# Gated window attention in one core: normalising in the input tile, transposes beside the maxima, mask first in the scores, key weights turned first, last output tile in two parts

## The chip, the cores and the metric

The kernel runs on one core of a Trainium2 chip. A core has five engines with a queue of their own: TensorE (PE in the profile; its weight loads are PEld), VectorE (DVE), ScalarE (ACT), GpSimd (POOL) and SyncE (SP), which here only issues DMAs. Matmuls write to PSUM, eight banks of 128 partitions x 512 f32. The metric is the device time of one execution in microseconds; less is better. Before the change it is 2263.09 us (median of 3 runs, 2261.22 to 2267.27).

## What is computed

For 8 sequences of 1024 tokens with 512 features, in f32:

```python
xn = (x - mean(x)) / sqrt(var(x) + 1e-5)
q, k, v = (heads(xn @ W.T + b) for W, b in ((Wq, bq), (Wk, bk), (Wv, bv)))   # 16 heads of 32
scores = q @ k.T / sqrt(32)
im = arange(1024) % 256
scores = where(im[:, None] >= im[None, :], scores, -1e30)
attn = softmax(scores) @ v
s = attn @ Wo.T + bo
y = clip((xn @ sign(weights).T) * scale + bias, -100, 100)
out = x + s * silu(y)
```

The mask goes by the place in a window of 256, not by the token's own place: a query sees, in each of the four windows, the keys up to its own place there.

## The kernel before

**Tiles.** Tokens are loaded so that a tile of 128 holds 32 places of all four windows (`tokens`, L124). In this order the mask is triangular over tiles: query tile i needs the key tiles 0 to i, and only the tile on the diagonal needs a mask inside. A batch has 8 tiles (`it`), 4 groups of 4 heads (`g`), and two halves of 4 tiles.

**Scores, twice.** For each batch and group the scores are made twice, each time in 9 quads: tiles of 4 banks, one bank a head, 4 heads side by side on 32 rows of TensorE each. There is one quad in PSUM (`ps_q`, one buffer), and all quads share it in turn.
- `maxima_quad` (L463, tile `s`): queries on partitions, keys along columns. S_QUADS says which queries and keys stand in each quad. The diagonal tile is masked by a product of two small bf16 matrices, `place_of` and `after` (L480), added to the scores in PSUM. VectorE takes the row maxima (L492). Five of the nine quads hold a diagonal; three of these hold two segments and two masks. The f32 product is L470.
- `shift_parts` and `shift_rows` split the maxima into three bf16 parts and transpose them (L519).
- `probs_quad` (L535, tile `t`): keys on partitions. First the shift is subtracted by a bf16 matmul (L541), then come the masks (L552), then the f32 product (L563). ScalarE takes Exp into a tile `p` (L576).
- `attend_quad` (L589) multiplies p with v into `av`; `add_probs` (L607) sums p on POOL; `sum_keys` (L630) sums over the keys; `invert` and `normalise_heads` divide (L664, L668).

**One step** of the main loop (from L948) is: the t quad of (b, g, n), the attend of the step before, a first fill, the s quad of the next group with the same n, a second fill. The fills are work that has nothing to do with the quad: projections q and k (`heads_work`), v (`values_work`), output tiles (`output_work`), gates (`gate_work`), transposes of xn (`turn` in `norm_work`). They keep TensorE at work while ScalarE does Exp (first fill) and VectorE the maxima (second fill). Two single banks (`ps_t`, `bank`) serve all of the fills, the turned maxima and the key sums.

**The plan.** The order of the fill is written out by hand in STEADY, OPENING and CLOSING (L726 to L743), one string for each group: V is a v tile, q20 the first half of q for group 2, k likewise, G a gate, O an output tile of the batch before, N the normalisation of a half of the next batch, W a turn of wo, a stroke marks work for the next batch, and what stands ahead of | may be taken early. Each word becomes a Block; `link` hangs smaller pieces on blocks some places away: an N at block i has its statistics at i - 5 and later (L777), its scale at i - 2 + half (L780), its normalising at i + half + 1 and later (L778), its turns at i + half + 2 + k (L779); a gate has its squash and finish behind it (L802, L803), an output tile its fetch one block ahead (L795). A `Work` has a cost (0.86 for a quarter of a product) and may be marked `edge` (run at the end of a fill, next to the quad), `late` (run at the end of the step) or `turn`. `Beside.fill` (L844) takes work from the front of the list until the wanted cost is reached. Work of cost 0 in the first fill is kept until after the s quad.

**Norms.** `stats` (L268) runs on VectorE, `scale` makes 1/sqrt on VectorE and POOL (L273 to L279), `normalise` makes xn in a buffer of the pool `tmp` (VectorE for the first batch, L284; ScalarE for the others, L289), and `turn` transposes it on TensorE into a bank (L301) that ScalarE copies into xnT (L302). `tmp` has 6 buffers of 128 x 512; gates (y, t), output tiles (s) and others draw on it too. `xpool` has 4 buffers for loaded tiles of x.

**Gates and outputs.** A gate's y is finished on POOL (L405, L406), for the last six (H in CLOSING) on VectorE; silu is made with Tanh, and the result g is stored to DRAM (L416). `output_work` fetches g and x again (L678, L680) into three buffers (`xres`), adds bo on VectorE (L686), multiplies by g and adds x on POOL (L688, L689; the last tile on VectorE) and stores (L690).

**Queues.** All loads of x, g and the stores go through SP in program order, so one that waits for a buffer or a result holds those behind it. In the opening wk and the biases go through ScalarE's queue.

**Beginning and end.** From L899: statistics of the first four tiles of x, normalise and turn them, turn wk (its copies alternate between VectorE and ScalarE, `evacuate` L223), then k, wq, q and so on, then the nine s quads of the first group with fill. From L1020: the last attend, then eight output tiles in the order 4 to 7, 0 to 3.

Of the kernel before, what the change touches and what calls it, by code (L numbers as in the profile page):

```python
# [9 lines left out]
F32 = mybir.dt.float32  # L10
# [7 lines left out]
B = 8  # L18
# [55 lines left out]
def tile_gated_window_attention(  # L74
# [23 lines left out]
    xpool = pool("xpool", 4)  # L98
# [7 lines left out]
    tmp = pool("tmp", 6)  # L106
# [123 lines left out]
    def turn_weight(name):  # L230


        def turn(c):
# [5 lines left out]
            ps = bank(f"{name}T_{c}")  # L239
# [4 lines left out]
            if name == "fw":  # L244

                sg = temp(f"sign_{c}")
                nc.vector.tensor_scalar(sg, ps, 0.0, 2.0, ALU.is_ge, ALU.mult)
                nc.vector.tensor_scalar(dst[:, c, :], sg, -1.0, None, ALU.add)
            elif name == "wo":

                nc.scalar.mul(dst[:, c, :], ps, 0.5)
            else:
                evacuate(dst[:, c, :], ps)
# [4 lines left out]
    xnT, turned = {}, set()  # L258

    def norm_work(b, half):  # L260
        its = range(4 * half, 4 * half + 4)
        mv, rstd, shift_by, xn = {}, {}, {}, {}
# [8 lines left out]
        def scale():  # L271
            rstd[0] = small.tile([P, 4], F32, tag="rstd", name=f"rstd_{b}_{half}")
            nc.vector.tensor_scalar(rstd[0], mv[0][:, :, 1], EPS, None, ALU.add)  # L273
            nc.gpsimd.tensor_tensor(rstd[0], rstd[0], neg_half, ALU.pow)
# [6 lines left out]
        def normalise(i, it):  # L281
            xn[it] = temp(f"xn_{b}_{it}")
            if b == 0:
                nc.vector.tensor_scalar(  # L284
                    xn[it], xt.pop((b, it)), mv[0][:, i, 0:1], rstd[0][:, i : i + 1],
                    ALU.subtract, ALU.mult,
# [3 lines left out]
                xn[it], xt.pop((b, it)), AF.Identity,  # L290
                bias=shift_by[0][:, i : i + 1], scale=rstd[0][:, i : i + 1],
            )

        def turn(i, it):
# [4 lines left out]
            x = xn.pop(it)  # L299
# [87 lines left out]
    def gate_work(b, it, plain=False):  # L387
# [13 lines left out]
        def after(ps):  # L401
            y[0] = temp(f"y_{b}_{it}")
            nc.vector.tensor_tensor(y[0], ps, rows["fscale"], ALU.mult)  # L403
            engine = nc.vector if plain else nc.gpsimd
            engine.tensor_tensor(y[0], y[0], rows["fbias"], ALU.add)  # L405
            engine.tensor_scalar(y[0], y[0], MAX_VAL, -MAX_VAL, ALU.min, ALU.max)  # L406
# [29 lines left out]
        if plain:  # L436
# [9 lines left out]
            Work(1.0, lambda: passes(0), edge=True),  # L446
            Work(1.0, lambda: passes(1), ready=lambda: bool(hold)),
        ]
        return split, [Work(2.0, both, lambda part: halves, edge=True)], squash, finish
# [13 lines left out]
    def maxima_quad(b, g, n):  # L463
        sc = quad(f"s_{b}_{g}_{n}")
        at = 0
        for i, lo, hi in S_QUADS[n]:
            own = lo <= i * P < hi
            w = hi - lo
            for h in range(NH):
# [4 lines left out]
                    start=(at == 0),  # L474
                    stop=not own,
                    skip_group_check=True,
                )
            if own:
                for h in range(NH):
                    nc.tensor.matmul(  # L480
                        sc[:, h, at + w - P : at + w],
                        lhsT=place_of[head_rows(h), :],
                        rhs=after[head_rows(h), :],
                        start=False,
                        stop=True,
                        skip_group_check=True,
                    )
# [187 lines left out]
    def output_work(b, it):  # L675
# [7 lines left out]
        def after(ps):  # L683
# [3 lines left out]
            engine = nc.vector if (b, it) == (B - 1, NT // 2 - 1) else nc.gpsimd  # L687
            engine.tensor_tensor(s, s, gb, ALU.mult)  # L688
            engine.tensor_tensor(s, s, xr, ALU.add)  # L689
            nc.sync.dma_start(tokens(out, b, it), s)  # L690

        main = product(
            f"o_ps_{b}_{it}",
            [
                (lambda g=g: (aT[b, g, it // 4][:, (it % 4) * P : (it % 4 + 1) * P], wT["wo"][:, g, :]))
                for g in range(NC)
            ],
            0.86,
            after,
        )  # L700
        return fetch, main

    def row_work():
# [7 lines left out]
        def after(ps):  # L711
# [3 lines left out]
            "bo_ps", [(lambda c=c: (wide[0][:, c, :], wT["wo"][:, c, :])) for c in range(NC)], 0.86, after  # L715
# [11 lines left out]
        "V4 G2 V5 | q20 V7 G3 V6 k20 q21 G4 k21",  # L727
        "O4 G5 O5 | q30 N0 k30 O6 q31 G6 k31 G7",
        "N1 O7 O0 | O1 k00' V0' q00' O2 q01' O3",
# [4 lines left out]
        "G3 G4 q20 G5 | N0 q30 k30 q31 G6 k31",  # L734
# [344 lines left out]
```

## Time and profile before

| what | value |
|---|---|
| median of the runs | 2263.09 us |
| the profiled execution | 2264.33 us |
| its span, first to last instruction | 2262.5 us |
| mean granted clock of TensorE | 0.997 |
| busy: TensorE, POOL, VectorE, ScalarE | 2200, 1467, 1208, 879 us |
| DMA moved | 93.51 MB, 41 GB/s over the span |
| Exp of one quad (L576) | 1.88 us |
| maxima of one quad of 4 x 512 (L492) | 2.29 us |
| one addition of 128 x 512 on POOL (L688) | 1.28 us |
| normalising one tile on ScalarE (L289) | 0.80 us |
| wait of TensorE for VectorE's first xn | 12.3 us |
| steady batch, from one to the next | 273.5 us |

The share of TensorE is that of time in which at least one matmul is in flight. Four matmuls of different heads run at once, so the starts of instructions tell more than their durations: the time that a group of matmuls takes from the stream is from its first start to the next group's first start. In the timeline's lines the columns are start, duration, engine, source line, operation, output<-inputs, shapes and number of instructions; in brackets stands the engine's idle time before it and what ended it. An f32 matmul shows as two instructions.

### The profile page before, as it was taken

The page shows a single profiled execution, that of the slowest core. Times are in us where ns is not written, and L with a number is a line of the kernel's source. Part 1 is how long each engine was busy: PE and PEld are TensorE (multiplying, and loading weights), DVE is VectorE, ACT ScalarE, POOL GpSimd, SP SyncE. Part 2 cuts the span into 40 slices and gives each one's busy share as a digit, 9 for nine tenths or more (in the row PEclk, how much of TensorE's full clock was granted, in tenths as well). Part 3 has the DMA queues.
Part 4 walks back from the last instruction along what each step waited for, and adds up shares of the span by engine and source line. Part 5 has one row for each costly group of instructions (what it writes and reads, how often), then busy time and mean ns, then how long its engine had stood idle before and what let it go on. Part 6 is the DMA issues. An engine that isn't in the chain of part 4 may idle for free.

```text
span 2262.5 us, 55901 instructions
## 1 busy us (share of the span) xinstructions
PE 2200.1 (97%) x25376; PEld 862.6 (38%) x25376; DVE 1207.5 (53%) x1535; ACT 879.2 (39%) x861; POOL 1467.1 (65%) x1291
## 2 busy tenths in 40 slices
PE   7999999999999999999999999999999999999998
PEld 3343433343433434333343333344333443333333
DVE  4555455564456544466455654555545664555563
ACT  2244433344333434344333443344344343333332
POOL 1367566776776766687567775667766676665663
PEclk9999999999999999999999999999999999999999
DMA  4001000121001210012000210002100111000123
GB/s 163 1 16 34 11 11 24 48 67 39 11 29 52 68 38 6 29 66 72 20 29 20 76 48 20 29 20 76 48 20 29 39 57 62 11 20 25 44 76 99
DMA packets 51087, 93.51 MB, mean 41 GB/s; under 512 B 6945, under 2 KB 6945, under 8 KB 50849
## 3 DMA queue, kind: packets, MB, share of 16 engines
q1 hardware_dynamic: 48720, 88.89, 11.9%
q8 instruction: 198, 3.24, 0.6%
q10 hardware_dynamic: 2128, 1.06, 0.2%
q14 instruction: 41, 0.33, 0.0%
HBM read 56.37 MB, written 33.55 MB: 40 GB/s over the span
## 4 chain that ended last, share of the span: by engine, by line
PE 83%; DVE 6%; ACT 4%; POOL 4%; issue 2%; DMA 1%; SPq 0%; ACTq 0%; POOLq 0%; DVEq 0%
PE s L470 13%; PE av L589 11%; PE t L563 10%; PE q_ps L331 9%; PE v_ps L331 9%; PE k_ps L331 9%; PE o_ps L331 7%; PE y_ps L425 5%; PE t L541 4%; DVE pm L492 4%; ACT p L576 2%; POOL p L607 2%; PE sum L630 2%; PE xnT_ps L301 2%; PE mT_ps L519 1%
## 5 line engine op out<-in xcount | busy, mean ns | idle before, releaser
L607 POOL TENSOR_TENSOR p<-p,p 128x512 f32<-128x512 f32 x930 | 1097.3, 1213 | 165.8 <-PE av L589 112.9
L492 DVE TENSOR_REDUCE pm<-s 128x4 f32<-128x2048 f32 (+3 forms) x384 | 665.1, 1753 | 709.9 <-PE s L480 462.6
L576 ACT ACTIVATE p<-t 128x2048 f32<-128x2048 f32 x288 | 540.8, 1878 | 760.8 <-PE t L563 684.7
L664 DVE RECIPROCAL aT<-aT 128x128 f32<-128x128 f32 x256 | 231.0, 929 | 242.8 <-ACT aT L625 242.8
L470 PE MATMUL s<-k,q 32*128 32x512 f32 (+3 forms) x3072 | 340.2, 528 | 15.4 <-ACT p L576 14.6
L589 PE MATMUL av<-p,v 128*32 128x512 f32 (+3 forms) x3072 | 308.7, 497 | 1.9 <-DVE aT L668 1.7
L563 PE MATMUL t<-q,k 32*128 32x512 f32 (+3 forms) x3072 | 305.6, 492 | 0.0
L331 PE MATMUL q_ps<-xnT,wqT 128*32 128x512 f32 (+3 forms) x2768 | 257.1, 486 | 4.5 <-ACT xnT L302 4.1
L331 PE MATMUL k_ps<-xnT,wkT 128*32 128x512 f32 (+3 forms) x2784 | 254.6, 483 | 0.3 <-ACT q L371 0.2
L331 PE MATMUL v_ps<-wvT,xnT 128*32 128x512 f32 (+3 forms) x2600 | 251.9, 505 | 0.0
L331 PE MATMUL o_ps<-woT,aT 128*32 128x512 f32 (+3 forms) x2480 | 249.1, 524 | 0.7 <-ACT xnT L302 0.7
L688 POOL TENSOR_TENSOR s<-s,gb 128x512 f32<-128x512 f32 x63 | 83.1, 1319 | 212.6 <-DVE s L686 211.5
L405 POOL TENSOR_TENSOR y<-y,fbias_r 128x512 f32<-128x512 f32 x58 | 76.4, 1317 | 201.8 <-DVE y L403 171.5
L399 POOL TENSOR_TENSOR x<-xnT,x 128x512 fp32r<-128x512 f32 x58 | 74.2, 1280 | 173.7 <-ACT x L398 169.9
L470 PEld LDWEIGHTS s<-k,q 32*128 32x128 f32 x3072 | 120.4, 183 | 134.2 <-ACT p L576 114.2
L563 PEld LDWEIGHTS t<-q,k 32*128 32x128 f32 x3072 | 138.4, 185 | 26.4
L331 PEld LDWEIGHTS q_ps<-xnT,wqT 128*32 128x32 f32 x2768 | 82.3, 110 | 170.9 <-issue 150.1
L589 PEld LDWEIGHTS av<-p,v 128*32 128x32 f32 x3072 | 70.3, 108 | 196.1 <-issue 161.1
L331 PEld LDWEIGHTS k_ps<-xnT,wkT 128*32 128x32 f32 x2784 | 83.5, 110 | 149.5 <-issue 125.2
L331 PEld LDWEIGHTS v_ps<-wvT,xnT 128*32 128x32 f32 x2600 | 75.1, 109 | 154.4 <-issue 139.1
L331 PEld LDWEIGHTS o_ps<-woT,aT 128*32 128x32 f32 x2480 | 74.0, 110 | 157.0 <-issue 144.8
L425 PE MATMUL y_ps<-fwT,x 128*128 128x512 f32 x464 | 129.4, 412 | 2.9 <-ACT q L371 2.9
(89 smaller groups left out, 1520.2 us busy)
## 6 DMA issues: line engine op xcount, KB each, us to landing
x<-in_L_attn_x_dram SPq DMA_DIRECT2D x64, 256.0 KB, 3.8
g<-t SPq DMA_DIRECT2D x64, 256.0 KB, 2.0
gb<-g SPq DMA_DIRECT2D x64, 256.0 KB, 3.0
xb<-in_L_attn_x_dram SPq DMA_DIRECT2D x64, 256.0 KB, 3.2
out_dram<-s SPq DMA_DIRECT2D x64, 256.0 KB, 2.5
wk_st<-in_L_attn_Wk_dram ACTq DMA_DIRECT2D x2, 512.0 KB, 4.6
wq_st<-in_L_attn_Wq_dram SPq DMA_DIRECT2D x2, 512.0 KB, 5.0
wv_st<-in_L_attn_Wv_dram SPq DMA_DIRECT2D x2, 512.0 KB, 6.6
```

Source lines behind the costliest of these rows:

```text
L331: nc.tensor.matmul(hold[0][cols, lo:hi], lhsT=lhsT[:, cols], rhs=rhs[:, lo:hi], start=(i == 0 and lo == 0), stop=(i == n - 1), skip_group_ ...
L405: engine.tensor_tensor(y[0], y[0], rows["fbias"], ALU.add)
L425: nc.tensor.matmul(hold[0], lhsT=part[i][:, c, :], rhs=wT["fw"][:, c, :], start=(i == 0 and c == 0), stop=(i == 1 and c == NC - 1),)
L470: nc.tensor.matmul(sc[:, h, at : at + w], lhsT=qt[b, g][head_rows(h), i * P : (i + 1) * P], rhs=kt[b, g][head_rows(h), lo:hi], start=(at = ...
L492: nc.vector.tensor_reduce(pm[:, 0 if lo == 0 else 1, i, :], sc[:, :, at : at + w], AX.X, ALU.max)
L541: nc.tensor.matmul(sc[:, h, at : at + w], lhsT=neg1[r, :], rhs=shift[b, g, f][r, lo : lo + w], start=(k == 0), stop=False, skip_group_chec ...
L563: nc.tensor.matmul(sc[:, h, at : at + w], lhsT=kt[b, g][head_rows(h), j * P : (j + 1) * P], rhs=qt[b, g][head_rows(h), q0 : q0 + w], start ...
L576: nc.scalar.activation(pt[:, :, :width], sc[:, :, :width], AF.Exp, scale=SCALE)
L589: nc.tensor.matmul(av[b, g, f][head_rows(h), lo : lo + w], lhsT=vt[b, j][:, g * P + h * DK : g * P + (h + 1) * DK], rhs=pts[b, g, n][:, h, ...
L607: nc.gpsimd.tensor_tensor(t[:, hs, lo : lo + w], t[:, hs, lo : lo + w], p[:, hs, at : at + w], ALU.add)
L664: nc.vector.reciprocal(r, r)
L688: engine.tensor_tensor(s, s, gb, ALU.mult)
```

## The change

- `normalise` writes xn back into the loaded tile of x. The tile is free when it has been turned, not when it has been normalised; `xpool` gets 5 buffers, `tmp` 5 in place of 6. A later load of x is ready only when the tile whose place it needs has been turned, a turn only when its tile is normalised.
- `scale` runs on POOL alone, and in the opening for two tiles at a time. For the second half of a batch statistics, scale and loads hang on other blocks.
- A turn is not run in a first fill, and at most one in a second. `fill` puts aside what is not ready if it is a turn or has no cost, and goes on with what follows; a product or a gate that is not ready ends the fill. Output tiles and gates get conditions (`ready`) of their own.
- The masks of an s quad are issued ahead of its f32 products, with the start flag.
- wk is turned ahead of everything else, into the four banks of the quad, and copied by ScalarE alone.
- The strings change: in STEADY q20 may be taken early, and O3 goes ahead of q01'; OPENING is rearranged. Turns of wo are marked `edge`. A gate's finish hangs one block earlier.
- The last gates use POOL as the others do. The last output tile has a function of its own: bo x g is added to x on POOL, the matmuls run in two halves of 256 columns, each is multiplied and added on VectorE and stored, one through SP, one through ScalarE's queue.

```diff
-    xpool = pool("xpool", 4)
+    xpool = pool("xpool", 5)
...
-    tmp = pool("tmp", 6)
+    tmp = pool("tmp", 5)
...
+            if name == "wk":
+
+                wide[0] = wide[0] or quad("wkT")
+                ps = wide[0][:, c, :]
+            else:
+                ps = bank(f"{name}T_{c}")
...
+            elif name == "wk":
+                nc.scalar.copy(dst[:, c, :], ps)
...
-        def scale():
-            rstd[0] = small.tile([P, 4], F32, tag="rstd", name=f"rstd_{b}_{half}")
-            nc.vector.tensor_scalar(rstd[0], mv[0][:, :, 1], EPS, None, ALU.add)
-            nc.gpsimd.tensor_tensor(rstd[0], rstd[0], neg_half, ALU.pow)
+        def scale(lo=0, hi=4):
+            if lo == 0:
+                rstd[0] = small.tile([P, 4], F32, tag="rstd", name=f"rstd_{b}_{half}")
+            r = rstd[0][:, lo:hi]
+            nc.gpsimd.tensor_scalar(r, mv[0][:, lo:hi, 1], EPS, None, ALU.add)
+            nc.gpsimd.tensor_tensor(r, r, neg_half[:, lo:hi], ALU.pow)
...
         def normalise(i, it):
-            xn[it] = temp(f"xn_{b}_{it}")
+            x = xt[b, it]
+            normed.add((b, it))
...
             nc.scalar.activation(
-                xn[it], xt.pop((b, it)), AF.Identity,
-                bias=shift_by[0][:, i : i + 1], scale=rstd[0][:, i : i + 1],
+                x, x, AF.Identity, bias=shift_by[0][:, i : i + 1], scale=rstd[0][:, i : i + 1]
             )
...
-            x = xn.pop(it)
+            x = xt.pop((b, it))
+            normed.discard((b, it))
...
-            engine = nc.vector if plain else nc.gpsimd
-            engine.tensor_tensor(y[0], y[0], rows["fbias"], ALU.add)
-            engine.tensor_scalar(y[0], y[0], MAX_VAL, -MAX_VAL, ALU.min, ALU.max)
+            nc.gpsimd.tensor_tensor(y[0], y[0], rows["fbias"], ALU.add)
+            nc.gpsimd.tensor_scalar(y[0], y[0], MAX_VAL, -MAX_VAL, ALU.min, ALU.max)
...
     def maxima_quad(b, g, n):
         sc = quad(f"s_{b}_{g}_{n}")
+        at, fresh = 0, False
+        for i, lo, hi in S_QUADS[n]:
+            w = hi - lo
+            if lo <= i * P < hi:
+                for h in range(NH):
+                    nc.tensor.matmul(
+                        sc[:, h, at + w - P : at + w],
+                        lhsT=place_of[head_rows(h), :],
+                        rhs=after[head_rows(h), :],
+                        start=not fresh,
+                        stop=False,
+                        skip_group_check=True,
+                    )
+                fresh = True
+            at += w
...
-                    start=(at == 0),
-                    stop=not own,
+                    start=not fresh,
+                    stop=True,
...
+    def last_output(b, it):
+
+        gb, xr = back.pop(it)
+        row = temp("row")
+        nc.gpsimd.tensor_tensor(row, gb, rows["bo"], ALU.mult)
+        nc.gpsimd.tensor_tensor(xr, xr, row, ALU.add)
+        s = temp(f"s_{b}_{it}")
+        ps = bank(f"o_ps_{b}_{it}")
+        for part, queue in enumerate((nc.sync, nc.scalar)):
+            at = slice(part * 256, part * 256 + 256)
+            for g in range(NC):
+                for h in range(NH):
+                    cols = head_rows(h)
+                    nc.tensor.matmul(
+                        ps[cols, at],
...
+            nc.vector.tensor_tensor(s[:, at], ps[:, at], gb[:, at], ALU.mult)
+            nc.vector.tensor_tensor(s[:, at], s[:, at], xr[:, at], ALU.add)
+            queue.dma_start(tokens(out, b, it)[:, :, at], s[:, at])
...
-        "V4 G2 V5 | q20 V7 G3 V6 k20 q21 G4 k21",
+        "V4 G2 V5 q20 | V7 G3 V6 k20 q21 G4 k21",
         "O4 G5 O5 | q30 N0 k30 O6 q31 G6 k31 G7",
-        "N1 O7 O0 | O1 k00' V0' q00' O2 q01' O3",
+        "N1 O7 O0 | O1 k00' V0' q00' O2 O3 q01'",
...
-        "G3 G4 q20 G5 | N0 q30 k30 q31 G6 k31",
-        "G7 N1 V0' V1' | W0 k00' W1 q00' W2 V2' W3 V3' q01'",
+        "G3 q20 q30 N0 k30 | G4 q31 G5 k31 G6 V0'",
+        "G7 N1 V1' | k00' q00' W0 V2' W1 V3' W2 q01' W3",
...
-                    link(i - 5 + 2 * half + k // 2, Work(0, stats[k], late=True))
+                    done = lambda key=(b + 1, 4 * half + k): key in normed
+                    link(i - 5 + (2 + k // 2 if half else 0) + k // 2, Work(0, stats[k], late=True))
                     link(i + half + max(1, k), normalise[k])
-                    link(i + half + 2 + k, Work(0.5, turn[k], turn=True))
-                link(i - 2 + half, Work(0, scale, late=True))
+                    link(i + half + 2 + k, Work(0.5, turn[k], turn=True, ready=done))
+                link(i - 2 + 2 * half, Work(0, scale, late=True))
...
-                link(i + 4 + later, finish)
+                link(i + 3 + later, finish)
...
-                    at = n0 + 4 + max(1, k)
-                    link(at, lambda b=b, it=4 + k: load_x(b + 1, it), True)
+
+                    ready = lambda key=(b + 1, k - 1): key[1] < 0 or key in turned
+                    fn = lambda b=b, it=4 + k: load_x(b + 1, it)
+                    link(n0 + 5 + k, Work(0, fn, ready=ready), True)
...
-                if not w.ready():
-                    if put_off:
-                        break
+                free = w.cost == 0
+                if not (free or w.turn or w.ready()):
                     while edge:
                         edge.pop(0).run()
-                if w.turn and (put_off or turns < 1):
+                if not w.ready() or free and waits or w.turn and turns < 1:
+                    if not (free or w.turn):
+                        break
+                    waits = waits or free
+                    turns = 0 if w.turn else turns
                     put_off.append(self.work.pop(0))
                     continue
...
+    for fn in turn_weight("wk"):
+        fn()
+    stats, scale, normalise, turn = norms[0]
+    for k in range(0, 4, 2):
+        stats[k]()
+        stats[k + 1]()
+        scale(k, k + 2)
+        normalise[k]()
+        normalise[k + 1]()
+    for k in range(4):
+        turn[k]()
     for w in heads_work(0, 0, 0, "k"):
         w.run()
+    stats, scale = norms[1][:2]
+    for k in range(0, 4, 2):
+        stats[k]()
+        stats[k + 1]()
+        scale(k, k + 2)
...
-                        want - spent, late, *kept, early=one is not now, turns=not (kept and turn)
+                        want - spent, late, *kept, early=one is not now, turns=not kept
...
+        if it == order[-1]:
+            last_output(b, it)
+            continue
```

## The prediction

> **What bounds the kernel now.** I read the page's busy times and its chain, then who waited for whom on TensorE, then the timeline of TensorE in one steady step.
>
> ```profile
> PE 2200.1 (97%) x25376; PEld 862.6 (38%) x25376; DVE 1207.5 (53%) x1535; ACT 879.2 (39%) x861; POOL 1467.1 (65%) x1291
> PE 83%; DVE 6%; ACT 4%; POOL 4%; issue 2%; DMA 1%; SPq 0%; ACTq 0%; POOLq 0%; DVEq 0%
> PE s L470 <- ACT p L576: 14.6, 13, 2.2
> PE xnT_ps L301 <- DVE xn L284: 12.3, 1, 12.3
> PE q_ps L331 <- ACT xnT L302: 4.1, 6, 0.7
> ```
>
> TensorE (PE) is busy 97% and carries 83% of the chain, so a microsecond taken out of its stream is gained, unless the loop through the one 4-bank quad becomes the limit. That loop is t (1.2 us), Exp (1.88), s (1.1), maxima (2.29) and a few tenths between, 6.9 us; a step now takes 273.5/36 = 7.6 us (the same stall recurs at 782.4, 1055.8, 1329.6, 1602.9 and 1876.7). So 0.7 us a step can go before the loop binds. The named waits are small, and most recur once a batch: they are the targets beside the stream itself.
>
> **Mask first.** The timeline of TensorE shows what a mask costs at the end of a score quad (s) and ahead of one (t, where it is so today). Columns: start, us, engine, line, tile.
>
> ```profile
> 1136.61 0.23 PE L552 MATMUL t<-place_of,after 32*128 32x128 bf16 x4
> 1136.67 1.08 PE L563 MATMUL t<-q,k 32*128 32x512 f32 x8
> 1137.68 1.07 PE L589 MATMUL av<-p,v 128*32 128x512 f32 x8
> 1138.56 1.37 PE L331 MATMUL v_ps<-wvT,xnT 128*32 128x512 f32 x16
> 1139.86 1.14 PE L470 MATMUL s<-k,q 32*128 32x512 f32 x8
> 1140.82 0.23 PE L480 MATMUL s<-after,place_of 32*128 32x128 bf16 x4
> 1140.98 0.75 PE L331 MATMUL v_ps<-wvT,xnT 128*32 128x320 f32 x8
> ...
> 1143.93 0.28 PE L552 MATMUL t<-place_of,after 32*128 32x128 bf16 x8
> 1144.05 1.09 PE L563 MATMUL t<-q,k 32*128 32x384 f32 x16
> 1145.07 1.06 PE L589 MATMUL av<-p,v 128*32 128x512 f32 x8
> 1145.95 1.58 PE L331 MATMUL k_ps<-xnT,wkT 128*32 128x320 f32 x24
> 1147.46 0.50 PE L470 MATMUL s<-k,q 32*128 32x128 f32 x8
> 1147.79 0.23 PE L480 MATMUL s<-after,place_of 32*128 32x128 bf16 x4
> 1147.85 0.88 PE L470 MATMUL s<-k,q 32*128 32x384 f32 x8
> 1148.55 0.23 PE L480 MATMUL s<-after,place_of 32*128 32x128 bf16 x4
> 1148.71 0.53 PE L331 MATMUL v_ps<-wvT,xnT 128*32 128x192 f32 x8
> ```
>
> Only starts count. A single masked s quad holds PE from 1139.86 to 1140.98, 1.12 us. The same work in t, mask first, takes 1136.67 - 1136.61 = 0.06 and then 1137.68 - 1136.67 = 1.01, together 1.07. I read the 0.05 as weight loading of q (183 ns, mean of the s weight-load row) that the first f32 pass now waits for in the open and that would run under the mask. A quad with two masks takes 1147.46 to 1148.71, 1.25 now; t with two masks first, 0.12 + 1.02 = 1.14, so 0.11 less. Of the nine quads of S_QUADS two have one mask and three have two: 2 x 0.05 + 3 x 0.11 = 0.43 us a (batch, group), x 32 = 13.8. The entry into the quad with a mask may cost a little: by starts a first mask takes 0.060 and a second 0.055, and 0.005 x 160 quads = 0.8. I take **-13**; ends 0 (nothing is hidden) and -15.
>
> [...]
>
> **Normalising in place.** L289 writes xn into a tmp buffer. Where six are in use, ScalarE waits, and Exp stands behind:
>
> ```profile
> 1326.95 0.81 ACT L289 ACTIVATE xn<-x,nmr,rstd 128x512 f32<-128x512 f32 x1 [5.98 <-POOL s L688]
> 1329.58 1.14 PE L470 MATMUL s<-k,q 32*128 32x512 f32 x8 [1.78 <-ACT p L576]
> ```
>
> This comes once a batch: s waited 2.20 (187.9), 1.08 (513.0), 1.56, 1.66, 1.78, 1.62 and 2.01 us, together 11.9. In the input tile there is no buffer to wait for. What could be late next is rstd: its scale moves a block later (i instead of i-1) and starts behind POOL's additions. In the batch shown these end at 1321.5, two output tiles follow to 1327.4; if scale's 1.7 us stands behind the first of them it is done by about 1326, and Exp of that step could start at 1325.6. So a few tenths may stay: **-11**; ends 0 (the wait only changes its name) and -12. The tile is now held until its transposes, so xpool has 5 and loads 5 to 7 of a half wait for turns; SP issues them when PE has transposed (1301.6 for the third), landing takes 3.8, and the statistics today start at 1296.6 to 1312 depending on the half: covered by several us. Behind these loads on SP stand the gb/xb fetches for two output tiles, which POOL needs only at 1321. tmp falls from 6 to 5, but loses up to four xn: nothing.
>
> **Turns only beside maxima, new order of blocks.** Today q01' follows O2, in which the last tile is turned, so the turn is flushed and PE waits 0.68 us for ScalarE's copy: five such waits in the steady batches, 3.4 us, and one of 0.7 before an output tile. With O3 between, 3.4 us of matmuls cover each: **-4**; ends 0 and -4.1. A change of the matmuls' shape costs about 0.11 us (1140.82 to 1140.98 is 0.16 for a mask of 0.05), in either fill, so moving a turn is worth nothing in itself. The waits for a bank at the turns (0.38, 0.27, 0.38) and before y (0.48), 1.5 us a batch, stay in kind; other places could remove or double them: 0, ends -9 and +9 for six batches. The four wo turns at edges spare a change of shape each, 4 x 0.1: **-0.4**. q20 may be taken early, and the gate's finish with its g store comes a block sooner; SP stands longest at that store (L416, 1123 us in 51 waits), and what it holds back, output fetches, is due later: 0, ends -2 and +2.
>
> **rstd on POOL.** L273 leaves DVE: 0.17 us, 1.23 at the longest, at 427.76, in front of the maxima for which PE then waited 2.01. **-1**; ends 0 and -2. POOL gets 16 x 0.23, beside 35% idle.
>
> **Opening.** wk lands by 1.17 + 5.6 = 6.8 us (its two landings took 3.6 and 5.6), its 16 transposes into four banks end near 11, ahead of xn. The statistics of x0 and x1 end at 8.1; scale on POOL 0.23 + 1.04 + gaps = 9.4; two normalisations at 0.54 end at 10.5; statistics of x2 and x3 2 x 0.87, 12.2; scale 13.5; two more 14.6; the last turn 0.66 and its copy 0.59, 15.9. k starts at 16.0 instead of 19.25: **-3.2**; ends 0 and -5.5 (statistics ahead of the first normalisations). wq lands by 9.81 + 5.4 = 15.2, before its turn at 19.5.
>
> **End.** The last tile's matmuls end at 2256.2, but its x is late: xb is issued at 2254.92, when POOL has freed a buffer, and arrives at 2258.25.
>
> ```profile
> 2254.92 0.54 SPq L680 DMA_DIRECT2D xb<-in_L_attn_x_dram  x1
> 2258.30 0.69 DVE L689 TENSOR_TENSOR s<-s,xb 128x512 f32<-128x512 f32 x1 [0.61 <-DMA xb<-in_L_attn_x_dram]
> ```
>
> Today one DVE addition of 0.69 follows, then the store (2259.01). The new tile first adds gb x bo to xb on POOL (1.28, to 2259.6), then DVE adds the first half, multiplies and adds the second: three times 0.42 (between 0.29 for 128 and 0.69 for 512 columns), 2260.9. The second store starts 1.9 us later than today's, and has half the bytes, worth 0.3: **+1.6**; ends -2 (x early) and +2.5.
>
> **Additions of the last gates on POOL.** Six gates give it 1.28 + 0.61 each, 11.4 us in a stretch of 67 where it is busy 46; DVE is relieved of 1.2 each, and at 2195 to 2198 such instructions stood ahead of the one PE waited 1.7 for. **0**; ends -1.5 and +4 (two Exp waiting for POOL's p one gate longer).
>
> **Sum.** -13 - 11 - 4 - 0.4 - 1 - 3.2 + 1.6 = -31.0. The profiled execution took 2264.3 (span 2262.5 and 1.8 around it), 1.2 above the median 2263.1; 2264.3 - 31.0 = 2233.3, on the median's level **2232**.
>
> **Rivals.** (1) *Hiding fails or a wait is replaced*: without the mask term 2245, or without the tmp term (rstd late on POOL) 2243. Against the first stand the t rows; for the second, POOL's backlog of 5.7 us there. Chance 0.22 for one of them. (2) *More goes than I count*: bank waits -9, opening -2 more, last group -1.5: 2219. Chance 0.09. (3) *Little happens*: two of the large terms fail and the bank waits double, -31 + 24 + 9 = +2, 2265, down to 2252 without the doubling and with one term half: 0.06. (4) *Slower*: the loads of the second half fall behind a held fetch on SP. Today SP stands from 1295.05 to 1322.81 at xb (L680), until POOL frees a buffer. If the load of x7 came behind it, it would land at 1326.6; its statistics, due near 1312, stand ahead of the maxima on DVE, and PE's next t waits some 14 us, in each of 7 batches: -31 + 98, 2330. It decides from (31 + 7)/7 = 5.4 us of uncovered landing a batch. Against it: the load's link lies ahead of the two fetches in the list, and what is put off keeps its order. Chance 0.08. The forecast itself, 2224 to 2240, 0.55.
>
> **The numbers.** A measurement here tells about 0.3% (7 us) from no change. The range 2219 to 2250 takes the forecast, (1) and (2), 0.86. Faster: 0.55 + 0.22 + 0.09 and a third of (3), 0.88; same 0.04; slower 0.08.
>
> **What would show it.** Right: masked quads of 1.07 and 1.14 us from start to next; no s waiting for p near the second step of group 2; q01' without its 0.68; k_ps starting near 16; last DVE addition near 2260.9 less the gain. Wrong: 0.53 us between f32 passes behind the mask; L289 waiting for rstd; DVE's statistics waiting for a DMA.

## The result and the profile after

The changed kernel takes 2277.01 us (median of 6 runs, 2273.75 to 2278.93) beside 2262.18 for the kernel before: the ratio is 1.0061, 95% interval 1.0048 to 1.0074. It is slower by 0.6%; the forecast was 2232. The profiled execution took 2278.93 (span 2277.1, granted clock 0.994).

The page of the changed kernel, busy times and chain of the work that ended last, by engine:

```profile
PE 2200.8 (97%) x25392; PEld 847.3 (37%) x25392; DVE 1189.0 (52%) x1506; ACT 880.1 (39%) x863; POOL 1487.9 (65%) x1325
PE 83%; DVE 9%; ACT 4%; POOL 2%; issue 1%; DMA 0%; POOLq 0%; SPq 0%; ACTq 0%; DVEq 0%
```

TensorE's busy time is what it was, although its weight loads fell by 15 us. What grew is VectorE's share of the chain, from 6% to 9%, while POOL's fell from 4% to 2%: the path now runs over VectorE in places where it did not. TensorE's waits say where (us in total, times, longest):

```profile
PE xnT_ps L311 <- DVE y L413: 11.9, 6, 2.2
PE xnT_ps L311 <- DVE s L700: 10.6, 6, 1.9
PE s L479 <- ACT p L590: 6.2, 5, 1.7
...
PE o_ps L341 <- ACT xnT L312: 3.4, 5, 0.7
```

The wait of s for p fell from 14.6 to 6.9 us (6.2 in quads with a mask, which now starts them, and 0.7 in those without), in the direction of the forecast. The first two lines are new: a turn (xnT_ps, L311) that waits for VectorE to empty a bank of y or of an output tile (s). They come to 22.5 us. Steps are counted from 0 here, as n is in the code. The timeline of TensorE at step 6 of group 1 in a steady batch:

```profile
1019.28 0.29 PE L479 MATMUL s<-after,place_of 32*128 32x128 bf16 x8
1019.41 1.08 PE L493 MATMUL s<-k,q 32*128 32x256 f32 x16
1020.42 1.20 PE L434 MATMUL y_ps<-fwT,x 128*128 128x512 f32 x4
1021.55 1.06 PE L341 MATMUL k_ps<-xnT,wkT 128*32 128x512 f32 x8
1024.81 0.66 PE L311 MATMUL xnT_ps<-ident,x 128*128 128x128 f32 x4 [2.19 <-DVE y L413]
...
1025.71 2.03 PE L577 MATMUL t<-q,k 32*128 32x512 f32 x8
```

The first two lines are a quad with two masks, masks first: 1020.42 - 1019.28 = 1.14 us, the figure of the forecast. Then the second fill makes the rest of a y and a part of k, in the two single banks, and the turn that ends the fill needs one of them. VectorE meanwhile:

```profile
1020.57 2.35 DVE L506 TENSOR_REDUCE pm<-s 128x4 f32<-128x1024 f32 x2 [6.11 <-PE s L493]
1022.84 0.18 DVE L520 TENSOR_REDUCE m<-pm 128x16 f32<-128x32 f32 x1
...
1023.97 0.23 DVE L520 TENSOR_REDUCE mt<-m 128x16 bf16<-128x32 f32 x1
1024.07 0.68 DVE L413 TENSOR_TENSOR y<-y_ps,fscale_r 128x512 f32<-128x512 f32 x1
```

The y in its bank was done on TensorE at 1021.6. VectorE takes it up at 1024.07, because the maxima (2.35 us) and, in this step, the seven reductions of `shift_parts` (1.2 us) stand ahead in its queue. The turn pays for both.

It pays twice. In TensorE's timeline above a t quad of eight passes takes 2.03 us after the wait, usually 1.08. Busy times by stretch (us; PE, PEld, DVE, ACT, POOL, then the granted clock, DMA's share and GB/s):

```profile
1022.00:1025.60 3.60, 1.41 (x16) 0.54 (x12) 3.43 (x12) 0.10 (x1) 0.88 (x2) 1.00 0.00 0
1025.60:1029.00 3.40, 3.40 (x32) 1.19 (x28) 0.73 (x2) 1.67 (x2) 3.31 (x4) 0.50 0.27 82
1029.00:1032.40 3.40, 3.40 (x40) 1.09 (x36) 0.66 (x1) 1.28 (x2) 0.27 (x1) 0.99 0.00 0
```

A stretch in which TensorE works 1.41 of 3.6 us is followed by 3.41 us at a granted clock of 0.5. TensorE is busy throughout, so I estimate the cost at half of it, 1.7 us. Before the end of the span there are four such stretches of 3.41 us in the kernel before; the changed one has eight times 3.41 us, two of them in one stretch.

### The profile page after: what moved, and what is told of

Read it like the earlier page. It is cut to its first block, busy times and chain, and to the rows that moved or that the text cites. A ratio compares the mean times of both kernels' runs of the same rounds, so it can differ in the third digit from the quotient of the medians.

```text
span 2277.1 us, 55996 instructions
## 1 busy us (share of the span) xinstructions
PE 2200.8 (97%) x25392; PEld 847.3 (37%) x25392; DVE 1189.0 (52%) x1506; ACT 880.1 (39%) x863; POOL 1487.9 (65%) x1325
## 4 chain that ended last, share of the span: by engine, by line
PE 83%; DVE 9%; ACT 4%; POOL 2%; issue 1%; DMA 0%; POOLq 0%; SPq 0%; ACTq 0%; DVEq 0%
PE s L493 11%; PE av L603 11%; PE t L577 11%; PE v_ps L341 9%; PE k_ps L341 9%; PE q_ps L341 8%; PE o_ps L341 7%; DVE pm L506 6%; PE y_ps L434 5%; PE t L555 4%; ACT p L590 2%; PE sum L644 2%; POOL p L621 2%; PE xnT_ps L311 2%; DVE aT L678 1%; PE s L479 1%
## 5 line engine op out<-in xcount | busy, mean ns | idle before, releaser
L493 PE MATMUL s<-k,q 32*128 32x512 f32 (+3 forms) x3072 | 320.3, 510 | 1.5 <-ACT q L381 0.8
L577 PE MATMUL t<-q,k 32*128 32x512 f32 (+3 forms) x3072 | 312.2, 501 | 0.0
L341 PE MATMUL o_ps<-woT,aT 128*32 128x512 f32 (+3 forms) x2504 | 243.7, 512 | 3.4 <-ACT xnT L312 3.4
L414 POOL TENSOR_TENSOR y<-y,fbias_r 128x512 f32<-128x512 f32 x64 | 83.5, 1304 | 222.0 <-DVE y L413 222.0
L341 PEld LDWEIGHTS k_ps<-xnT,wkT 128*32 128x32 f32 x2640 | 78.9, 110 | 154.8 <-issue 133.4
L493 PEld LDWEIGHTS s<-k,q 32*128 32x128 f32 x3072 | 116.2, 185 | 48.4 <-ACT p L590 39.8
```

The costliest lines, as they stand in the source:

```text
L341: nc.tensor.matmul(hold[0][cols, lo:hi], lhsT=lhsT[:, cols], rhs=rhs[:, lo:hi], start=(i == 0 and lo == 0), stop=(i == n - 1), skip_group_ ...
L414: nc.gpsimd.tensor_tensor(y[0], y[0], rows["fbias"], ALU.add)
L493: nc.tensor.matmul(sc[:, h, at : at + w], lhsT=qt[b, g][head_rows(h), i * P : (i + 1) * P], rhs=kt[b, g][head_rows(h), lo:hi], start=not f ...
L577: nc.tensor.matmul(sc[:, h, at : at + w], lhsT=kt[b, g][head_rows(h), j * P : (j + 1) * P], rhs=qt[b, g][head_rows(h), q0 : q0 + w], start ...
```

## The experiments

**Theory** (the bank): a turn confined to the second fill waits for a bank behind VectorE's maxima; that, with the clock it costs, is what made the kernel slower. **Rivals**: the masks first cost more elsewhere than they save; the opening or the end cost it; the in-place tile or the loads do.

### Four runs on where the time went

e1: the kernel before with the new `maxima_quad` alone.

> The kernel before with the score masks first and nothing else. Bank theory (the changed kernel loses its time where a turn beside the maxima waits for a bank that VectorE empties only behind its maxima, and in the half clock that follows; masks first are a gain): 160 masked quads, 96 of them 0.104 shorter and 64 of them 0.045 (medians of the changed kernel's starts, 1.14 against 1.25 and 1.08 against 1.13), 13 us less: 2249, between 2247 and 2252. Rival (the stream itself got worse by the masks): 2262 or more.

2249.82 us, ratio to before 0.9944 (0.9929 to 0.9959). The theory's number holds, the rival falls. Not all of it is the mask: before the end this profile (granted clock 0.999) has one half-clock stretch where the kernel before (0.997) has four, 3 x 1.7 = 5 us by the estimate above, which come and go with the timing. That the sum hit the forecast's 13 so closely is in part luck.

e2: the changed kernel with the old rule for turns. `kept` is there in a first fill alone, and `turn` in steps 0 and 7 alone, so the old rule keeps turns out of two of the nine first fills of a group and the new one out of all.

```diff
-turns=not kept
+turns=not (kept and turn)
```

> The changed kernel, but a turn may again run in a first fill where no maxima are turned. Bank theory: the turn at the 7th step of group 1 goes back to a place where VectorE is free, so of the two waits of 2 us a batch at least that one goes, with the half clock behind it (about 1.6): 3.6 us or more a batch in 5 to 6 batches, 2250 to 2258. Rival (the time is lost through tiles of x held longer, later loads and scale on POOL, which stay): 2274 to 2279.

2249.67 us, 0.9946 (0.9931 to 0.996): one condition takes back 27 us. The group 1 of a steady batch goes from 72.52 us (70.91 to 74.06 in five of them) to 66.58. The turn's wait for y, 11.9 us, is down to one of 0.9:

```profile
PE xnT_ps L311 <- DVE y L413: 0.9, 1, 0.9
```

These 11.0 us and half clock spared (four times 3.41 us less, 6.8 by the estimate; the granted clock is 0.997 beside 0.994) make 18 of the 27. The rest is spread over smaller waits; one of them the rule had brought in by itself, 0.68 us of an output tile for ScalarE's copy of xnT in each steady batch (3.4 us in the changed kernel and in e3, 0.7 in the kernel before and in e2). The turn's wait for s stays at 10.2 us.

e3: the reverse, the kernel before with turns only beside the maxima.

```diff
-turns=not (kept and turn)
+turns=not kept
```

> The kernel before, in which a turn may run only in a second fill; nothing else. Bank theory: one or two waits of about 2 us a batch come in, each with up to 1.7 us of half clock: 2280 to 2305. Rival (the rule is harmless, the loss comes from the held tiles): 2258 to 2266.

2271.40 us, 1.0042 (1.0027 to 1.0057). The sign is the theory's, the size (+9) is not. The new wait is there in full, 10.8 us of xnT_ps for y in 5 times; but TensorE's wait of s for p fell from 14.6 to 6.5 us. Perhaps standing still in group 1 gave the tiles of `tmp` time to come free; no run shows it.

e4: the changed kernel with `shift_parts` issued after the second fill.

```diff
             maxima_quad(*nxt, n)
-            if n == 6:
-                shift_parts(1)
-            if n == 8:
-                shift_parts(0)
...
             fill(max(share, 2.35) - spent)
+            if n == 6:
+                shift_parts(1)
+            if n == 8:
+                shift_parts(0)
```

> The changed kernel, with the seven small reductions of the maxima (1.4 us on VectorE at the 7th and 9th step) issued after the second fill, so that y and s are taken out of their banks before them. Bank theory: both waits of 2 us shrink by 1.4 to some 0.6, too short for the half clock: 2 x (1.4 + 1.6) a batch in 5 to 6 batches, 2240 to 2250. Rival (held tiles): 2274 to 2280.

2250.86 us, 0.995 (0.9933 to 0.9966), 26 us less than the changed kernel with the turns where the change has them. TensorE and VectorE at the same step as above:

```profile
1017.37 0.66 PE L311 MATMUL xnT_ps<-ident,x 128*128 128x128 f32 x4 [0.95 <-DVE y L413]
...
1018.25 1.08 PE L577 MATMUL t<-q,k 32*128 32x512 f32 x8
```

```profile
1014.37 2.35 DVE L506 TENSOR_REDUCE pm<-s 128x4 f32<-128x1024 f32 x2 [6.12 <-PE s L493]
1016.64 0.68 DVE L413 TENSOR_TENSOR y<-y_ps,fscale_r 128x512 f32<-128x512 f32 x1
```

With the seven reductions behind y the wait falls from 2.19 to 0.95 us, and the t quad takes 1.08 again: no half clock is left before the last tiles (granted clock of the span 0.999, where the changed kernel has 0.994). The bank theory stands: the turns' place, and the order of VectorE's queue, each take the loss away without touching anything else of the change.

### Four runs on the other parts

e5 and e6 were to combine e2's group 1 with e4's group 2. e6 was also to have the turns of batches 0 and 1 in either fill, and has the old last tile.

```diff
 e5, on e4:
-turns=not kept
+turns=not (kept and g == 1)
 e6, on e5: the same with (b < 2 or g == 1), and the old last tile
```

> The changed kernel with the seven reductions of shift_parts issued after the second fill (as in e4), and a turn kept out of the second fill in group 1 alone; in the other groups a turn still stands only beside the maxima. Bank theory, now read step by step: in a steady batch group 1 took 66.58 us with turns beside either fill (e2) and 69.67 with turns beside the maxima (e4), group 2 took 72.83 or 71.25 and 68.06 in the same two kernels; groups 0 and 3 stood at 68.35 and 66.0 in both. So a steady batch should take 68.35 + 66.58 + 68.06 + 66.0 = 269.0 us in place of 272.07 in e4, and none of its waits on a y_ps or o_ps bank should be above 1 us, so that the clock stays at 1.0. Five to six batches gain 3 us each: 2231 to 2237 us. Rival: the work beside one group only moves the waits of the next (what group 1 gains, group 2 loses, since the late turns of group 1 were what delayed the rest): 2247 to 2253, as e2 and e4.

> e5 with two more edits: in batches 0 and 1 turns stand beside either fill in all groups, as in e2, whose batches 0 and 1 took 272.7 and 263.5 us where e4's took 278.1 and 268.1; and the last tile is done as in the kernel before (one product, VectorE for its gate and sum). From the last t quad to the end of the span the kernel before took 39.25 us and two kernels with its tail 38.95 and 39.17, the changed kernel 40.57 and e2 40.59. Theory: 5.4 + 4.7 us from batches 0 and 1 and 1.4 from the tail, 11 below e5: 2220 to 2227 us. Rival, that what the first two batches gain returns as waits in the third, and that the tail of 40.6 comes from the run and not from the last tile: the same as e5 within 3 us.

The edit has the wrong sense: where the bracket is true the *first* fill takes no turn, so group 1 keeps its turns beside the maxima and the other groups are freed, the opposite of what both expectations say (in e6 batches 0 and 1 keep theirs too). e5 took 2250.39 us, 0.994 (0.9925 to 0.9954), and its steady batches are e4's to 0.05 us, so, with `shift_parts` late, the rule matters in group 1 alone of a steady batch. e6 took 2247.76, 0.993 (0.9915 to 0.9945); from the last t quad to the end its span has 38.99 us, e5's 41.61, the changed kernel's 40.57 and the kernel before's 39.25. The end of e5 holds a half-clock stretch (granted clock of its span 0.999). The last tile in two parts itself costs 1.3 us by the changed kernel beside the kernel before, and 1.7 by e2 (40.59) beside e9 below (38.88), which has the old one.

e7: the kernel before with the new opening (its scale still begins on VectorE).

> The kernel before with only the new opening: the key weights turned first of all through one quad, the first four tiles scaled two by two, x 4 to 7 measured after the first key product. The forecast's term was -3.2 us. In the profiles of three kernels with the new opening the first t quad started at 81.17, 79.42 and 79.31, in three with the old one at 80.60, 80.35 and 80.32. Theory: -1.1 us where the clock rises as early as in the old opening, and +0.7 where it rises one window of 3.41 us later (the first key product then took 5.46 in place of 3.64): 2260 to 2263 beside the kernel before at 2262. Rival, the forecast's own term: 2258.5 to 2259.5.

2263.53 us, 1.0002 (0.9993 to 1.0012): nothing, the forecast's -3.2 falls. TensorE in the opening of the changed kernel:

```profile
9.52 1.11 PE L247 MATMUL wkT<-ident,wk_st 128*128 128x128 f32 x4 [2.03 <-ACT wkT L259]
...
18.39 5.46 PE L341 MATMUL k_ps<-xnT,wkT 128*32 128x512 f32 x32 [0.68 <-ACT xnT L312]
```

Each turn of wk waits for ScalarE's copy of the bank before (2.03, 0.68 and 0.68 us), though they go into four banks of one quad; ahead of the first copy ScalarE loads a table (ACT_TABLE_LOAD, 1.28 us from 7.59). The transposes take 1.11 where later ones take 0.66. The first product starts at 18.39, not at 16.0, and takes 5.46 us where the kernel before has 3.64. In twelve profiles with this opening the full clock is first recorded at 16.8 to 18.4 us in six and at 22.0 to 22.7 in six, and the first t quad starts at 79.1 to 79.6 and 81.1 to 81.5; in five with the old opening at 15.8 to 18.4, and 79.8 to 80.6. What the earlier product gains was lost again in half of the profiles; that the clock rises there one window of 3.41 us later, as the expectation has it, was not shown.

e8: e2 with xn in a tile of its own.

```diff
-            x = xt[b, it]
+            x = xt.pop((b, it))
+            xn[it] = temp(f"xn_{b}_{it}")
```

> e2 (the changed kernel with turns beside either fill) with xn back in a tile of its own from tmp (pool sizes as before). Theory: in-place normalisation is what took the wait of the second step of group 2 away (8.99 us before, 7.26 in e2), so it returns in six batches: +1.7 us each, 2257 to 2262 us. Rival: the wait went because of the new order of the blocks or of the new half-1 loads, and the buffer does nothing: 2248 to 2252, as e2.

2251.27 us, 0.9948 (0.9932 to 0.9964), the same as e2. My theory fell: beside the earlier finish and the later scale, which stay, the input tile buys nothing.

### Seven runs on the wait for a buffer, and on the best version

By the code a gate's two tiles of `tmp` are given back when its `finish` runs, and the change links that one block earlier.

e9: e2, `shift_parts` late as in e4, old last tile.

> The changed kernel with turns beside either fill (as in e2), the seven reductions of shift_parts after the second fill (as in e4) and the last tile as in the kernel before. In e2 a steady batch took 66.58 us in group 1 and 71.25 to 72.83 in group 2, in e4 69.67 and 68.06; groups 0 and 3 were the same in both. Bank theory: the late reductions shorten the wait of 2.05 us at the sixth step of group 2 to about 0.7, as they did in e4, and take the half clock behind it away. If group 2 takes 68.06, five batches gain 20 us on e2 and the tail 1.6: 2227. If the three waits for a copy of k, v and q at steps 3 to 5 of group 2 (0.38, 0.28, 0.38, there in e2 and not in e4) stay, a batch takes about 270.6 and the time is 2236. So 2226 to 2238. Rival: the waits only move again and the steady batch stays at 272: 2246 to 2250.

2233.90 us, 0.987 (0.9855 to 0.9885), inside the expected span: the three waits of turns for ScalarE's copies (0.38, 0.27 and 0.38 us) stayed, and the steady batch is 270.83. Waits of xnT_ps for s, with e2 first (10.2 us, half-clock stretches in batches 2, 4 and 6) and then e9:

```profile
PE xnT_ps L311 <- DVE s L700: 10.2, 5, 2.0
```

```profile
PE xnT_ps L311 <- DVE s L700: 4.0, 5, 0.8
```

e10 and e11: the late finish again, on e8 (xn in tmp) and on e2 (xn in place). e12: the kernel before with the early finish alone, the same line edited the other way.

```diff
-                link(i + 3 + later, finish)
+                link(i + 4 + later, finish)
```

> e8 (xn back in a tile from tmp, turns beside either fill, 2251.3 us) with the gate's finish again one block later, as in the kernel before. Theory, new: the wait of the second step of group 2 was for the y and t tiles of a gate, which the earlier finish gives back 9 us sooner (15.76 against 24.82 us from the start of group 2 in e8 and e1), and not for xn's own place. Then the wait of 1.7 us is back in each of six batches: 2259 to 2263. Rival: the later scale or the new order of the output tiles took the wait away: 2249 to 2253, as e8.

> e2 (xn in its input tile, turns beside either fill, 2249.7 us) with the gate's finish again one block later. Theory: in-place normalisation or the earlier finish, either one alone, takes the wait of the second step of group 2 away; in place, xn asks for no tmp buffer, so the wait does not come back: 2248 to 2252. Rival: the earlier finish is the only remedy, since the tiles of y, t and s then wait for each other in a pool that is one smaller: 2257 to 2262.

> The kernel before with one number changed: the gate's finish (and its store) linked three blocks after the gate in place of four. Theory: this alone takes the wait of s for p at the second step of group 2 away, 1.7 us in six batches, and nothing is added: 2250 to 2255. Rival: it needs the later scale too, or the finish stands in front of something else on VectorE: 2259 to 2266.

e10 took 2253.85 us, 0.9961 (0.9949 to 0.9974): the wait did not come back, the theory fell. e11 took 2251.62, 0.9949 (0.9937 to 0.9962), as e2. e12 took 2245.53, 0.9924 (0.9912 to 0.9937): one number brings 18 us. Its wait of s for p:

```profile
PE s L470 <- ACT p L576: 4.1, 4, 1.7
```

That is 10.5 us less than the 14.6 of the kernel before; and none of the four half-clock stretches before the end is left (granted clock 1.000 beside 0.997), 4 x 1.7 = 6.8 by the estimate. In a steady batch the second normalisation, which waited 5.98 us for a buffer in the kernel before, follows the first at once:

```profile
1310.05 1.51 ACT L289 ACTIVATE xn<-x,nmr,rstd 128x512 f32<-128x512 f32 x2
```

That it is the gate's tiles which it gets is read from the code; the trace shows that the wait goes.

e13: the kernel before with mask first and early finish. e14: e10 with the scale at `i - 2 + half` again, one block earlier for the second half. e15: e10 with the old order of blocks (q20 behind the bar, q01' between O2 and O3).

> The kernel before with two edits alone: the mask first in the score quads (e1, -12.8 us) and the gate's finish one block earlier (e12, -18.0 us against its own runs of before). Theory: the two have nothing in common, one shortens TensorE's stream and the other ends a wait, so they add: 2262.5 to 2263.5 less 30.8 is 2232 to 2233, with 270.3 us a steady batch; bounds 2229 to 2236. Then nothing else in the change pays. Rival: part of what the earlier finish brings is the half clock that it spares, which e1 spared already (e1 had two such stretches, the kernel before five): three of them at 1.7 us would be counted twice, 2236 to 2240.

> e10 (the changed kernel with turns beside either fill, xn in tmp and the late finish, 2253.9 us, and still no wait at the second step of group 2) with the scale of the second half again in the block where the kernel before has it, one earlier. Theory: in e10 it is the late scale that holds xn back until a buffer is free (the first xn stood for POOL's scale until 15.1 us after the start of group 2), so Exp is no longer behind a wait for a buffer; with the early scale the wait of 1.7 us is back in five or six batches: 2261 to 2265. Rival: the order of the output tiles does it: 2252 to 2256, and group 2's second step at 7.26.

> e10 with the old order of the blocks (q20 after the bar of group 0, q01' between the output tiles O2 and O3). Theory (late scale is the remedy in e10): group 2's second step stays at 7.26; the wait of the turn for o_ps at the sixth step (2.05 us) becomes the 0.68 of q01' for the copy, so 1.2 us a batch less and no half clock behind it: 2242 to 2248. Rival: the order of the output tiles is the remedy: the second step is back at 8.99 in five batches, 2251 to 2256.

e14 took 2261.41 us, 0.9994 (0.9984 to 1.0003), as its theory had it. ScalarE in group 2 of a steady batch, in e14 and then in e10:

```profile
1039.65 0.80 ACT L300 ACTIVATE xn<-x,nmr,rstd 128x512 f32<-128x512 f32 x1
1045.92 0.81 ACT L300 ACTIVATE xn<-x,nmr,rstd 128x512 f32<-128x512 f32 x1 [5.46 <-POOL s L702]
1046.64 1.85 ACT L591 ACTIVATE p<-t 128x2048 f32<-128x2048 f32 x1
```

```profile
1041.92 1.52 ACT L300 ACTIVATE xn<-x,nmr,rstd 128x512 f32<-128x512 f32 x2 [3.64 <-POOL nmr L289]
1043.72 1.88 ACT L591 ACTIVATE p<-t 128x2048 f32<-128x2048 f32 x1 [0.28 <-PE t L578]
```

With the early scale the second xn waits 5.46 us for a buffer and Exp stands ready behind it (no wait of its own is shown). With the late one the first xn waits for POOL's scale; by then a buffer is free, both run, and Exp waits 0.28 us for its t, for nothing else. (The third xn of e10 still waits 4.13 us for a buffer, but TensorE's step there is 7.86 us as in the kernel before.) e15 took 2244.73 us, 0.992 (0.9905 to 0.9934), 9 less than e10: with q01' between the output tiles step 2 of group 2 stays at 7.26 us and step 6 goes from 9.78 to 8.55, without the turn's wait for s. So the new order of blocks costs 9 us while the turns are free.

e13 took 2236.93 us, 0.9883 (0.9867 to 0.99). That is its rival's span, 4 to 5 us above the plain sum, which fits three half-clock stretches (3 x 1.7 = 5.1 us by the estimate) that e1 and e12 both counted. By e12's and e13's profiles the mask alone is 1.44 us in a steady batch and 9.7 over the span. e9 and e13 can't be told apart; both beat the kernel before by over 1%, and e13 does so with two edits. All that the change has besides these two costs 40 us (2277.0 - 2236.9). The rule for turns (27), the order of blocks (9) and the last tile (1.3), each measured in a plan of its own, make 37 of them; the other 3 were not traced.

## Why the prediction was wrong

| term | forecast | measured |
|---|---|---|
| mask first | -13 | -12.8 (e1); -9.7 of it without the half clock (e12 to e13) |
| normalising in place | -11 | 0 beside the two other remedies (e8 beside e2); alone not run |
| finish one block earlier | 0, -2 to +2 | -18.0 alone (e12) |
| new order of blocks | -4 | +9 with the turns free (e15 to e10) |
| turns only beside maxima | 0, -9 to +9 | +27 (e2); +9 in the old plan (e3) |
| opening | -3.2 | 0 (e7) |
| last tile | +1.6 | +1.3 to +1.7 |

rstd on POOL, the clips of the last gates on POOL and the wo turns at edges (-1, 0 and -0.4) were not run by themselves.

**The step that failed** is "A change of the matmuls' shape costs about 0.11 us ..., in either fill, so moving a turn is worth nothing in itself", with "The waits for a bank at the turns ... stay in kind ...: 0, ends -9 and +9". I priced the bank waits from the turns' old places (0.27 to 0.48 us, ScalarE's copies) and allowed them to double. At the new place another engine frees the bank, and its queue holds the maxima: 2.35 us, in two steps of nine with `shift_parts` behind them. A line in my own text gave 2.29 us for the maxima, and the second fill is by construction the time they take. I had not asked who empties the bank that the moved instruction needs, and what that engine does in just that fill. Of the 45 us between the forecast (2232) and the result, 27 are this term and 13 the order of blocks below.

**The multiplier that I left out** is the clock. Four half-clock stretches stood in the profile before, and I passed over its 0.997. By the estimate they cost 6.8 us there (4 x 1.7), the eight times 3.41 us of the changed kernel 13.7, and one turns a wait of 2 us into 3.7.

**Right, but not for the reason given**: the wait of L289 for a buffer went; in the changed kernel no normalisation (L299) has idle time before it. It had asked for one buffer of `tmp` at one moment, and the change has three remedies for it: no buffer asked for (in place), one given back sooner (early finish), the asking later (late scale). In the new plan the late scale alone suffices: e10 has neither of the others, and when it is undone too (e14) the wait returns, 7.6 us dearer. In the old plan the early finish alone suffices (e12). In place alone was run in neither plan, so what it would have brought stays open. I put it all on in place and priced the early finish at nothing because I looked for its cost on SP, not for the tile it holds.

**The new order**: the 0.68 us of q01' was seen rightly and did go; but with O3 next to the turn the bank it needs is an output tile's, behind the same maxima: 2.05 us (e2). In e15, which has the old order, this wait is gone and the 0.68 is back.

**The opening** failed on a wait that I did not count, of a turn for the copy of another bank in the same quad (the last turn of wk starts at 13.10, where I had all of them end near 11), and on TensorE's pace in the opening, where a transpose of wk takes 1.11 us (later ones 0.66) and the first product 5.46 (3.64 in the kernel before).

**The last tile** came as forecast: POOL's addition for it ends at 2272.52, and VectorE's three times 0.42 behind it at 2273.76; the tail is 1.3 us longer where 1.6 was forecast. The last store, with half the bytes, takes 3.3 us to the end of the span beside 3.5 before; the 0.3 that the forecast gave for the bytes was an estimate without a row behind it, and the two half stores landed in 2.1 and 2.2 us where whole ones take 2.5 (median).

**The rivals**: none was this one. (4) foresaw a slower kernel by a held fetch on SP; no statistics of the steady batches waited for a DMA. (3) had "the bank waits double", in kind the nearest, at 9 us. Hiding did not fail either: by the medians of starts e1's quads with one mask took 1.082 us where they had taken 1.127, those with two 1.144 and 1.140 where they had taken 1.246 and 1.243. In the changed kernel's timeline the weight load for q/k (L493) begins at 1019.35, while the two masks ahead of it run (1019.28 to 1019.57).

## What to carry to other kernels

Before moving an instruction of TensorE, ask for the bank it will write: who empties it, and what stands ahead in that engine's queue at the new place; a fill made as long as the maxima is a bad place for an instruction that needs VectorE. When a wait for a buffer is to go, list everyone who holds a buffer of the pool, and for how long: giving one back a block earlier (one number) brought 18 us by itself. And when a change has several remedies for one wait, its gain is counted once.

## What the runs showed of the hardware

In the profile of the kernel before each of the four half-clock stretches ahead of the end lasts 3.41 us; in that of the changed kernel six last 3.41 us and one, from 1855.1, lasts 6.83, with TensorE busy for 6.67 of it. A wait of about 2 us does not always draw one: in e2 the same wait of 2.05 us, once a batch, drew it in batches 2, 4 and 6 and not in 3 and 5. What sets these apart no run shows. The three batches with it took 273.74 to 273.81 us, the two without 272.17: 1.6 us, close to the 1.7 that I estimated.
